# Transform products and transposes on 128x32 tiles, with two moves in the order of VectorE and ScalarE

## The chip, the cores and the metric

The kernel runs on one core of a Trainium2 chip. The metric is the device time of one execution in microseconds (us). A core has five engines that work side by side, each through its own queue in order: TensorE (PE in the profile, its weight loads apart as PEld), VectorE (DVE), ScalarE (ACT), GpSimd (POOL) and SyncE (SP). POOL and SP mostly issue DMA transfers here. All data is fp32.

## The reference

Input x is 8 images of 32 channels and 128 x 128 pixels. Two layers follow one another, each with a normalisation of channel pairs ahead and a residual sum behind:

```
layer 0:  g  = groupnorm(x)                           16 groups of two channels
          for 25 offsets in a 5x5 window: cost = 3x3 box sum of sum_c (g - shifted g)^2
          idx = the 8 offsets of least cost, per pixel
          xb  = the 8 shifted copies of g              256 channels, c*8 + k
          dct = for each c: 8x8 matrix over k of xb    (a grouped 1x1 convolution)
          h   = relu(dw3x3(W1 xb));  h = relu(dw3x3(W3 h));  w = sigmoid(dw3x3(W5 h))
          x1  = x + Wagg * (grouped 8->1 of (w * dct))
layer 1:  out = x1 + conv5x5(groupnorm(x1))            one 5x5 kernel for all channels
```

W1, W3 and W5 are 256 x 256; dw3x3 is a convolution of each channel with its own 3x3 kernel. "Transform" below is the line dct, "convolution 1, 2, 3" the three pairs of a 1x1 and a 3x3 convolution.

## The kernel before

An image goes through in 16 strips of R = 8 rows, with one further round (n = 16) that empties the pipeline. The main loop runs over 136 steps (8 images x 17), and each step has four stages in the order i = 3, 2, 1, 0: convolution 3 of strip s-2, convolution 2 of strip s-1, convolution 1 of strip s, and the transform and final sum of strip s-2. The 256 channels lie as two tiles of 128 partitions.

*A convolution.* The upper 128 channels are done on VectorE: `pointwise_v` makes the 1x1 products (pv, in PSUM), ScalarE copies them to tv (L678), ScalarE makes the first of nine taps (L722) and VectorE the other eight as multiply-adds of 128 x 1024 elements (L725); ScalarE applies the activation (L729). `depthwise_v` is a generator for this: its successive `next` calls give the first tap, the eight multiply-adds, the activation, and the DMA that moves the last two rows to the top for the next strip (`rows_before_v`, on SP). The lower 128 channels are done on TensorE: `pointwise_t` (p), ScalarE's copies to t (L701), row copies on SP (L707, L709), and `depthwise_t` makes the 3x3 convolution as products with small diagonal weights (pw, L751), with the activation in the copy out (L764).

*The order.* PE, DVE and ACT take their instructions in the order in which the program calls them; it is written by hand in the main loop. `new_v` is the generator of the running stage, `dv` that of the stage before, `kept` that of the one before that. So the activation of convolution 1 is issued at the end of stage 0 (`next(dv, None)`), and its row copy in stage 3 of the next step (`next(kept, None)`). The block matching for the next image (squares of differences on DVE and ACT, df; sums on PE, pd; the 8 best by MAX8 and FIND_INDEX8, L536 and L537; indices, oc) is cut into small tasks in queues "D", "A", "P" and "Q"; `tick` takes a share of the D tasks in each stage.

*The gather.* Each stage builds one selection: POOL loads indices (ib, L602), ScalarE makes one-hot rows in two passes (sel, L616 and L617), and PE multiplies them with pixels (pg, L631), copied to xb (L638) and from there to DRAM (xbd, L640).

*Transform and final sum.* `final_load` (at the end of stage 0, for the next step) brings the residual rows xr and the matched strips xf back from DRAM. For xf it issues eight DMAs of 32 partitions (L791), so that the partitions are ordered by the half of the channels; xf has one buffer, so the load waits for the last reader. `final_dct` multiplies xf with ldct in 64 x 64 quadrants: four products fill the quadrants for four rows of both tiles, eight for a full strip (pc, L810). VectorE multiplies the convolution 3 result by them (L818). In the next step `final_add` makes the products pa with the aggregation weights (L831), VectorE adds xr (L839) and takes statistics (L840), and POOL stores the rows (L844).

*PSUM.* pv, p, pg, pc, pa and the transposes share the pool ps_x of five buffers, handed out in turn; pc takes four of them in a full step. pw and pd have their own.

*Transposes.* Pixels (px, L407, four per group, 64 groups), costs (pt, L525, the same) and indices (pi, L569, 64 singly) are turned by TensorE's transpose of 128 x 128 tiles.

Of the kernel before, what the change touches and what calls it, by code (L numbers as in the profile page):

```python
# [8 lines left out]
F32 = mybir.dt.float32  # L9
# [7 lines left out]
P = 128  # L17
C, K, H, W = 32, 8, 128, 128
# [18 lines left out]
C_M32 = C_G2 + 32  # L37
# [7 lines left out]
def bm3d_conv_preact(  # L45
# [16 lines left out]
    nc = tc.nc  # L62
# [41 lines left out]
    lw5 = const.tile([P, 2, CK], F32, name="lw5")  # L104


    ldct = const.tile([P, 2, 64], F32, name="ldct")
    lagg = const.tile([P, 2, C], F32, name="lagg")


# [89 lines left out]

    queues = {"B": deque(), "D": deque(), "A": deque(), "P": deque(), "Q": deque()}

# [94 lines left out]
    def mixes():  # L300

        dq = work.tile([P, 2, K], F32, name="dq", tag="dq", bufs=1)
        src = dct_w.rearrange("(m h c i) k a b -> m h k c (i a b)", m=2, h=2, i=K)
        for k in range(K):
            for m in range(2):
                for h in range(2):
                    p = 64 * h + 32 * (k % 2) + 8 * (k // 2)
                    nc.sync.dma_start(dq[p : p + 8, m], src[m, (h + m + 1) % 2, k])
        m8 = work.tile([P, 8], F32, name="m8", tag="m16", bufs=1)
        yield "D", 1.0, 10  # L310
        nc.vector.tensor_reduce(
            m8,
            cst[:, C_M32 : C_M32 + C].rearrange("p (a c) -> p c a", c=8),
            axis=mybir.AxisListType.X,
            op=ALU.add,
        )
        for m in range(2):
            nc.vector.tensor_tensor(
                ldct[:, m].rearrange("p (c i) -> p c i", i=K),
                m8.unsqueeze(2).to_broadcast([P, 8, K]),  # L320
                dq[:, m].unsqueeze(1).to_broadcast([P, 8, K]),
                ALU.mult,
            )

# [74 lines left out]
    def sources(b, xn):  # L399
# [3 lines left out]
        for r in range(0, 32, 4):  # L403
            yield "P", 0
            pt = ps_x.tile([P, 4, P], F32, name=f"px_{b}_{r}", tag="x")
            for q in range(4):
                nc.tensor.transpose(pt[:, q], xn[:, 3 + r + q, 2 : 2 + W], ident)  # L407
            xs = work.tile([P, 4, P], F32, name=f"xs_{b}_{r}", tag="ct")
            nc.scalar.copy(xs, pt)
            for q in range(4):  # L410
                nc.gpsimd.dma_start(
                    xl.rearrange("(g r) x c -> r x g c", g=4)[r + q],
                    xs[:, q].rearrange("p (g c) -> p g c", c=C),
                )
# [70 lines left out]
    def costs(b, i, sq, idx):  # L485
# [35 lines left out]
        for h in range(0, R, 4):  # L521
            yield "P", 0
            pt = ps_x.tile([P, 4, P], F32, name=f"pt_{b}_{i}_{h}", tag="x")
            for q in range(4):
                nc.tensor.transpose(pt[:, q], cost[:, h + q], ident)  # L525
# [16 lines left out]
    def places(b, idx, i):  # L542
# [23 lines left out]
        yield "P", 0  # L566
        for h in range(2):
            pt = ps_x.tile([P, 512], F32, name=f"pi_{b}_{i}_{h}", tag="x")
            nc.tensor.transpose(pt[:, :P], o[:, h * P : (h + 1) * P], ident)  # L569
# [141 lines left out]
    def depthwise_v(i, b, n):  # L711
# [4 lines left out]
        for k, (dy, dx) in enumerate(  # L716
# [4 lines left out]
            if k == 0:  # L721
                nc.scalar.activation(acc, rows, AF.Copy, scale=tap)  # L722
                yield out_
            else:
                nc.vector.scalar_tensor_tensor(  # L725
                    acc, rows, tap, acc, op0=ALU.mult, op1=ALU.add
                )
# [42 lines left out]
    def final_load(b, n):  # L770
# [24 lines left out]

    def final_dct(b, n, acc, xf, j0, j1):

        for r0 in range(0, R, 4):
# [5 lines left out]
            pc = [  # L804
                ps_x.tile([P, 4, W], F32, name=f"pc_{b}_{n}_{m}_{r0}", tag="x") for m in range(2)
            ]
            for h in range(2):
                for m in range(2):
                    o = 64 * ((h + m + 1) % 2)
                    nc.tensor.matmul(  # L810
                        pc[m][o : o + 64, : z - a],
                        ldct[64 * h : 64 * h + 64, m],
                        xf[64 * h : 64 * h + 64, m, a:z],
                        start=True,
                        stop=True,
                    )
# [219 lines left out]
    with tc.manual_schedule(engines=ORDERED):  # L1036
# [19 lines left out]
        for s in range(len(steps) + 2):  # L1056
# [10 lines left out]
            for i in (3, 2, 1, 0):  # L1067
# [111 lines left out]
```

## Time and profile before

| | |
|---|---|
| median of 3 runs | 6524.21 us (6519.26 to 6526.59) |
| the profiled execution | 6526.97 us, its span 6525.2 us |
| TensorE's granted clock over the span | 0.979 of full speed |
| busy: PE / PEld / DVE / ACT / POOL | 6180.3 / 3262.3 / 5856.5 / 5051.0 / 3077.3 us |
| multiply-adds of the convolutions on VectorE (L725) | 4031.6 us, 3264 instructions |
| transform products (L810, pc) | 272.0 us of 64x512, 1984 records |
| transpose products px, pt, pi | 42.6, 44.5, 15.5 us |
| xf loads issued by POOL (L791) | 651.0 us, 1088 instructions |

Columns of a group in the profile: line, engine, operation, output <- input with buffer numbers left out, partitions x elements, count, then busy time, mean of one in ns, and the idle time of the engine just before, with the instruction that ended most of it. For products the partitions are given as rows * columns of the part of the array in use (128*32 is 128 rows by 32 columns). Products overlap, so the mean of one is longer than what it adds. The list of waits has the waiting line, the line waited for, us in total, times, and the longest. The view of stretches gives the length of each, and the busy time of each engine in it.

### The profile page before, as it was taken

To read this page: it belongs to the slowest core of one execution; us is meant where nothing else is said; L and a number is where in the kernel's file an instruction comes from. 1 tells how busy PE (TensorE), PEld (TensorE's weight loads), DVE (VectorE), ACT (ScalarE), POOL (GpSimd) and SP (SyncE) were. 2 spreads that over 40 slices of the span, in tenths; PEclk is the share of its full clock that TensorE was granted. 3 is DMA by queue.
4 is the path that set the end of the run, shared out by engine and by line. 5 is a ranking of instruction groups with operands and counts; after the bars stand their busy time and mean duration, and the time that the engine had idled before them with its cause. 6 is when DMAs were issued, how large, how long until landed. Compare 5 with 4: busy or idle time off the path is not lost.

```text
span 6525.2 us, 234180 instructions
## 1 busy us (share of the span) xinstructions
PE 6180.3 (95%) x102306; PEld 3262.3 (50%) x102306; DVE 5856.5 (90%) x8828; ACT 5051.0 (77%) x6698; POOL 3077.3 (47%) x5015
## 2 busy tenths in 40 slices
PE   5799999999999999999999999999999999999997
PEld 1445445544555546454555544544545454465553
DVE  7899988999889998899998999899998999988776
ACT  5787769778787877877778787887869787787772
POOL 8345436444364444643446534454345644344334
PEclk7899999999999999999999999999999999999998
DMA  4555555565555655655546556565555665455553
GB/s 85 125 135 144 123 124 146 145 143 135 133 145 139 142 147 127 150 140 135 141 129 157 140 131 151 127 150 137 139 134 138 150 147 133 118 149 147 137 135 79
DMA packets 544960, 886.21 MB, mean 136 GB/s; under 512 B 248880, under 2 KB 312944, under 8 KB 543936
## 3 DMA queue, kind: packets, MB, share of 16 engines
q0 software_dynamic: 383648, 611.87, 37.4%
q1 hardware_dynamic: 157776, 258.11, 16.4%
q8 instruction: 805, 13.19, 0.9%
q10 hardware_dynamic: 2512, 1.25, 0.1%
q14 instruction: 219, 1.79, 0.1%
HBM read 420.60 MB, written 216.49 MB: 98 GB/s over the span
## 4 chain that ended last, share of the span: by engine, by line
PE 50%; DVE 32%; ACT 5%; POOL 5%; DMA 4%; issue 4%; SPq 0%; ACTq 0%; DVEq 0%; POOLq 0%
DVE acc L725 21%; PE pw L751 16%; PE pv L670 12%; PE p L694 11%; PE pg L631 4%; DVE idx L537 3%; POOL xtd L424 3%; PE pc L810 2%; DVE df L444 2%; DVE acc L818 1%; PE p L924 1%; DVE mx L536 1%; PE pd L459 1%; DMA t<-t 1%; ACT sel L616 1%
## 5 line engine op out<-in xcount | busy, mean ns | idle before, releaser
L725 DVE SCALAR_TENSOR_TENSOR acc<-tv,dwv,acc 128x1024 f32<-128x1024 f32 (+3 forms) x3264 | 4031.6, 1237 | 156.3 <-ACT acc L722 52.0
L751 PE MATMUL pw<-t,dwd 96*32 96x254 f32 (+7 forms) x31680 | 2118.1, 419 | 23.0 <-DMA t<-t 10.1
L751 PEld LDWEIGHTS pw<-t,dwd 96*32 96x32 f32 (+1 forms) x31680 | 1105.7, 110 | 826.8 <-issue 369.3
L616 ACT ACTIVATE sel<-ib,nplace 128x1024 f32<-128x1024 uint8 x1024 | 1170.8, 1143 | 62.0 <-DMA ib<-idxd 62.0
L617 ACT ACTIVATE sel<-sel 128x1024 f32<-128x1024 f32 x1024 | 1086.0, 1061 | 32.5
L670 PE MATMUL pv<-acc,lw 128*32 128x512 f32 x8448 | 959.8, 590 | 54.4 <-DVE acc L818 47.8
L694 PE MATMUL p<-acc,lw 128*32 128x256 f32 x16768 | 974.3, 379 | 2.2 <-issue 2.2
L602 POOL DMA_DIRECT2D ib<-idxd x512 | 292.0, 570 | 1207.3 <-ACT sel L616 1078.1
L791 POOL DMA_DIRECT2D xf<-xbd x1088 | 651.0, 632 | 279.9 <-PE pc L810 180.6
L694 PEld LDWEIGHTS p<-acc,lw 128*32 128x32 f32 x16768 | 570.7, 111 | 393.6 <-issue 67.4
L729 ACT ACTIVATE acc<-acc 128x1024 f32<-128x1024 f32 (+3 forms) x408 | 417.1, 1022 | 390.2 <-DVE acc L725 389.8
L678 ACT COPY tv<-pv 128x512 f32<-128x512 f32 (+2 forms) x784 | 435.9, 579 | 338.5 <-PE pv L670 334.1
L631 PE MATMUL pg<-sel,xt 120*32 120x88 f32 (+1 forms) x24576 | 611.7, 244 | 64.8 <-ACT sel L617 56.1
L631 PEld LDWEIGHTS pg<-sel,xt 120*32 120x32 f32 x24576 | 559.5, 111 | 219.2 <-ACT sel L617 74.4
L670 PEld LDWEIGHTS pv<-acc,lw 128*32 128x32 f32 x8448 | 290.2, 110 | 532.3 <-issue 409.7
L764 ACT ACTIVATE acc<-pw 128x512 f32<-128x512 f32 (+2 forms) x808 | 436.6, 572 | 133.4 <-PE pw L751 131.8
L444 DVE TENSOR_TENSOR df<-xn 128x786 f32<-128x786 f32 (+2 forms) x576 | 530.4, 972 | 2.2 <-PE pd L459 1.9
L701 ACT COPY t<-p 128x512 f32<-128x512 f32 x800 | 421.7, 571 | 115.4 <-PE p L694 115.4
L452 ACT ACTIVATE df<-df 128x786 f32<-128x786 f32 (+2 forms) x576 | 458.9, 859 | 50.0 <-DVE df L444 48.6
L722 ACT ACTIVATE acc<-tv,dwv 128x1024 f32<-128x1024 f32 (+3 forms) x408 | 455.1, 1115 | 42.3 <-PE pa L831 24.8
L670 PE MATMUL pv<-xb,lw 128*32 128x512 f32 x4096 | 470.8, 596 | 0.0
L694 PE MATMUL p<-xb,lw 128*32 128x256 f32 x8192 | 469.9, 380 | 0.0
(155 smaller groups left out, 5893.0 us busy)
## 6 DMA issues: line engine op xcount, KB each, us to landing
ib<-idxd POOLq DMA_DIRECT2D x512, 256.0 KB, 4.0
xbd<-xb POOLq DMA_DIRECT2D x128, 1024.0 KB, 6.0
xf<-xbd POOLq DMA_DIRECT2D x960, 128.0 KB, 6.8
t<-t SPq DMA_DIRECT2D x792, 128.0 KB
t<-t SPq DMA_DIRECT2D x384, 256.0 KB
tv<-tv SPq DMA_DIRECT2D x384, 130.0 KB
xt<-xtd POOLq DMA_DIRECT2D x240, 180.0 KB, 4.0
xtd<-xl POOLq DMA_DIRECT2D x192, 96.0 KB, 3.3
```

Source lines behind the costliest of these rows:

```text
L444: nc.vector.tensor_sub(df[:, :, ca:cz], xn[:, r0 : r0 + SR, ca:cz], xn[:, r0 + dy : r0 + dy + SR, ca + dx : cz + dx],)
L452: nc.scalar.activation(df[:, :, ca:cz], df[:, :, ca:cz], AF.Square)
L616: nc.scalar.activation(sel, ib, AF.Square, bias=nplace)
L617: nc.scalar.activation(sel, sel, AF.Relu, scale=-1.0, bias=1.0)
L631: nc.tensor.matmul(pg[C * j : C * (j + 1), :, :, xa:xz], xt[: 8 * QW, f * (NT // 2) + t], sels[j // 2][: 8 * QW, j % 2 * 2 : j % 2 * 2 + 2 ...
L670: nc.tensor.matmul(ps[C * j : C * (j + 1), :hr], lhsT[:, g, P + C * j : P + C * (j + 1)], src(g)[:, h : h + hr], start=g == 0, stop=g == 1,)
L694: nc.tensor.matmul(ps[C * r : C * (r + 1), e, :nb], lhsT[:, g, s], rows[:, r : r + 4 * nb - 3 : 4], start=g == 0, stop=g == 1,)
L722: nc.scalar.activation(acc, rows, AF.Copy, scale=tap)
L725: nc.vector.scalar_tensor_tensor(acc, rows, tap, acc, op0=ALU.mult, op1=ALU.add)
L751: nc.tensor.matmul(pt[u][C * j : C * (j + 1), ka:kz, :nb, xa:xz], dwd[0:hi, i - 1, u, j, dx + 1], t[0:hi, j, ka:kz, :nb, xa + dx : xz + dx ...
L764: nc.scalar.activation(rows[:, u : u + 2 * nh[u] - 1 : 2, :nb], pt[u][:, : nh[u], :nb], funcs[i - 1])
L791: nc.gpsimd.dma_start(xf[p : p + C, m, j0:j1], src[g, m, (h + m + 1) % 2, :, :, ya:yz])
```

## The change

There are four parts. (1) The transform is made with 128 x 32 column tiles: ldct holds the whole 128 x 128 block matrix of a tile, xf is loaded in the order of xbd's partitions with two DMAs of 128 partitions, and each of two tiles and four column blocks is one product over all 128 rows. (2) The transposes of px, pt and pi become four ordinary products each, with 32 columns of the data as weights and the identity as the moving operand. (3) In convolution 1, the multiply-adds stop after six; the transform's VectorE products come next, and then the last two multiply-adds. (4) Convolution 1's activation is issued in stage 3 of the next step, right behind the first tap of convolution 3, and not at the end of stage 0.

```diff
-    ldct = const.tile([P, 2, 64], F32, name="ldct")
+    ldct = const.tile([P, 2, P], F32, name="ldct")
...
+    def transpose(out_, in_):
+        for j in range(0, P, C):
+            nc.tensor.matmul(out_[j : j + C], in_[:, j : j + C], ident, start=True, stop=True)
...
     def mixes():
-        src = dct_w.rearrange("(m h c i) k a b -> m h k c (i a b)", m=2, h=2, i=K)
+        src = dct_w.rearrange("(m c i) k a b -> m k c (i a b)", m=2, i=K)
         for k in range(K):
             for m in range(2):
-                for h in range(2):
-                    p = 64 * h + 32 * (k % 2) + 8 * (k // 2)
-                    nc.sync.dma_start(dq[p : p + 8, m], src[m, (h + m + 1) % 2, k])
+                p = 32 * (k // 2) + k % 2
+                nc.sync.dma_start(dq[p : p + 31 : 2, m], src[m, k])
...
-                nc.tensor.transpose(pt[:, q], xn[:, 3 + r + q, 2 : 2 + W], ident)
+                transpose(pt[:, q], xn[:, 3 + r + q, 2 : 2 + W])
...
-                nc.tensor.transpose(pt[:, q], cost[:, h + q], ident)
+                transpose(pt[:, q], cost[:, h + q])
...
-            nc.tensor.transpose(pt[:, :P], o[:, h * P : (h + 1) * P], ident)
+            transpose(pt[:, :P], o[:, h * P : (h + 1) * P])
...
     def depthwise_v(i, b, n):
             else:
+                if i == 1 and k == 7:
+                    yield
                 nc.vector.scalar_tensor_tensor(
...
     def final_load(b, n):
-        src = xbd[b].rearrange("(j m h c) g y x -> g m h j c y x", j=4, m=2, h=2)
+        src = xbd[b].rearrange("(j m c) g y x -> m j (c g) (y x)", j=4, m=2)
         for m in range(2):
-            for h in range(2):
-                for g in range(2):
-                    p = 64 * h + C * g
-                    nc.gpsimd.dma_start(
-                        xf[p : p + C, m, j0:j1], src[g, m, (h + m + 1) % 2, :, :, ya:yz]
-                    )
+            nc.gpsimd.dma_start(
+                xf[:, m, j0:j1].rearrange("p y x -> p (y x)"), src[m, :, :, W * ya : W * yz]
+            )
...
     def final_dct(b, n, acc, xf, j0, j1):
-            for h in range(2):
-                for m in range(2):
-                    o = 64 * ((h + m + 1) % 2)
+            for m in range(2):
+                for q in range(4):
+                    s = slice(C * q, C * (q + 1))
                     nc.tensor.matmul(
-                        pc[m][o : o + 64, : z - a],
-                        ldct[64 * h : 64 * h + 64, m],
-                        xf[64 * h : 64 * h + 64, m, a:z],
+                        pc[m][s, : z - a],
+                        ldct[:, m, s],
+                        xf[:, m, a:z],
                         start=True,
                         stop=True,
                     )
...
                     accs[i, bi, ni] = [None, next(new_v)]
+                if i == 3:
+                    next(kept, None)
                 next(later, None)
...
                     final_dct(bi, ni, accs[3, bi, ni], xf, j0, j1)
+                if not i:
+                    next(dv, None)
...
                 run("A")
-                next(dv, None)
+                if i:
+                    next(dv, None)
```

In the main loop's stage 0 `dv` is the generator of convolution 1, so the new `next(dv, None)` issues its last two multiply-adds behind `final_dct`; in stage 3 of the next step `kept` is the same generator, and the new `next(kept, None)` issues its activation, the old one its row copy. Convolutions 2 and 3 keep their order.

More of the change, by code (lines that the diff above doesn't have):

```diff
@@ L302, in mixes @@
         dq = work.tile([P, 2, K], F32, name="dq", tag="dq", bufs=1)
-        src = dct_w.rearrange("(m h c i) k a b -> m h k c (i a b)", m=2, h=2, i=K)
+        src = dct_w.rearrange("(m c i) k a b -> m k c (i a b)", m=2, i=K)
         for k in range(K):
             for m in range(2):
-                for h in range(2):
-                    p = 64 * h + 32 * (k % 2) + 8 * (k // 2)
-                    nc.sync.dma_start(dq[p : p + 8, m], src[m, (h + m + 1) % 2, k])
-        m8 = work.tile([P, 8], F32, name="m8", tag="m16", bufs=1)
+                p = 32 * (k // 2) + k % 2
+                nc.sync.dma_start(dq[p : p + 31 : 2, m], src[m, k])
+        m16 = work.tile([P, 16], F32, name="m16", tag="m16", bufs=1)
         yield "D", 1.0, 10
         nc.vector.tensor_reduce(
-            m8,
-            cst[:, C_M32 : C_M32 + C].rearrange("p (a c) -> p c a", c=8),
+            m16,
+            cst[:, C_M32 : C_M32 + C].rearrange("p (c g) -> p c g", g=2),
             axis=mybir.AxisListType.X,
@@ L319, in mixes @@
                 ldct[:, m].rearrange("p (c i) -> p c i", i=K),
-                m8.unsqueeze(2).to_broadcast([P, 8, K]),
-                dq[:, m].unsqueeze(1).to_broadcast([P, 8, K]),
+                m16.unsqueeze(2).to_broadcast([P, 16, K]),
+                dq[:, m].unsqueeze(1).to_broadcast([P, 16, K]),
                 ALU.mult,
```

## The prediction

> **What bounds the kernel now.** I read first the page's engine row and its chain, then TensorE's own timeline of one step with the products' shapes, then what TensorE waits for, and last the steps one by one. From the page:
>
> ```profile
> span 6525.2 us, 234180 instructions
> ...
> PE 6180.3 (95%) x102306; PEld 3262.3 (50%) x102306; DVE 5856.5 (90%) x8828; ACT 5051.0 (77%) x6698; POOL 3077.3 (47%) x5015
> ...
> PE 50%; DVE 32%; ACT 5%; POOL 5%; DMA 4%; issue 4%; SPq 0%; ACTq 0%; DVEq 0%; POOLq 0%
> ```
>
> TensorE leaves 345 us of the span open, VectorE 669; the chain changes between the two. TensorE's timeline of a step (start, length, group; a group runs on for some 0.2 us under the next, so its cost is start to next start):
>
> ```profile
> 3004.51 3.63 PE L670 MATMUL pv<-acc,lw 128*32 128x512 f32 x32
> 3007.94 0.86 PE L459 MATMUL pd<-df,neg 128*32 128x396 f32 x8
> ...
> 3018.17 3.64 PE L670 MATMUL pv<-xb,lw 128*32 128x512 f32 x32
> 3021.75 0.66 PE L525 MATMUL pt<-cst,dsum 128*128 128x128 f32 x4
> 3022.34 3.66 PE L694 MATMUL p<-xb,lw 128*32 128x256 f32 x64
> ...
> 3026.76 5.31 PE L751 MATMUL pw<-t,dwd 96*32 96x512 f32 x48
> 3032.00 1.95 PE L810 MATMUL pc<-xf,ldct 64*64 64x512 f32 x16
> 3033.88 0.86 PE L459 MATMUL pd<-df,neg 128*32 128x393 f32 x8
> ...
> 3042.17 3.64 PE L670 MATMUL pv<-acc,lw 128*32 128x512 f32 x32 [1.32 <-DVE acc L818]
> ```
>
> To see: the line of pv has 16 products of the code as 32 records, two per fp32 product, and takes 3.43 us from start to next start: eight rounds of four records, 0.43 us each. The transform, pc, has 8 products, 16 records, in 1.88 us: four rounds of 0.43 and a rest. What pv waits for in the last line is a result buffer: pc holds four of the five x buffers until VectorE's multiplications (L818) have read them, and these stand behind eight multiply-adds of convolution 1:
>
> ```profile
> 3031.01 10.51 DVE L725 SCALAR_TENSOR_TENSOR acc<-tv,dwv,acc 128x1024 f32<-128x1024 f32 x8
> 3041.43 2.47 DVE L818 TENSOR_TENSOR acc<-acc,pc 128x512 f32<-128x512 f32 x4
> ```
>
> TensorE's waits from 230 to 6420 us (before that VectorE and ScalarE prepare image 0, after it the last image is finished):
>
> ```profile
> PE pv L670 <- DVE acc L818: 47.8, 28, 3.6
> PE pg L631 <- ACT sel L617: 46.9, 28, 2.2
> PE pi L569 <- DVE oc L560: 31.6, 10, 8.6
> PE pc L810 <- ACT t L701: 12.3, 7, 2.4
> ```
>
> By the stretches of that view TensorE's open time is 109 us before 230, 45 after 6420 and 191 between; only the 191 can be won here. Then each step of image 3, from pc to the next pc (length, then busy time of TensorE, weight loads, VectorE):
>
> ```profile
> 2937.10:2987.10 50.00, 50.00 (x821) 24.18 (x820) 41.69 (x47) 38.88 (x51) 18.57 (x27) 1.00 0.53 126
> ...
> 3032.00:3080.60 48.60, 45.40 (x778) 23.10 (x774) 47.09 (x80) 37.63 (x50) 13.11 (x24) 1.00 0.49 121
> ...
> 3218.10:3268.20 50.10, 45.31 (x755) 23.49 (x754) 48.27 (x105) 34.72 (x47) 21.27 (x38) 0.97 0.61 141
> ...
> sum 791.80, PE 766.63 PEld 406.73 DVE 729.18 ACT 630.06 POOL 382.65; mean PE 45.10 PEld 23.93 DVE 42.89 ACT 37.06 POOL 22.51
> ```
>
> The first step is TensorE's alone: no gap, and VectorE has 8 us over. In the other two VectorE waits for nothing; its 1.5 to 1.8 us beside the busy time are the small gaps between its instructions. TensorE is the limit in most steps, VectorE in about five of seventeen.
>
> **The change, part by part.** *Transform.* pc becomes 16 products of 128 rows by 32 columns, over all 128 rows though only 32 of them carry weights for a block of columns: 32 records of 128x512, the very shape of pv, so 3.43 us. Now it costs 1.88 plus its way in: the pw group ahead takes 5.24 us to pc's start, where the 96-record group with the same columns takes 5.16 (3013.01 to 3018.17), so 0.1. That is +1.45 per full step. The way in and out of the 64*64 tiles (0.1, and 1.88 - 4 x 0.43 = 0.16) is all that the new shape saves; the four extra rounds are 1.72. There are 8 x 15 full steps: 174 us. The first step of an image (5 rows) has 5/8 of the rounds, +0.8; the last (3 rows) +0.37: 9 us. Sum 183.
>
> *Transposes.* A group of four pt or px is 4 records now, 0.59 us, plus 0.15 on its way in (3018.17 to 3021.75 is 3.58, against 3.43). As ordinary products it is 16 products, 32 records, eight rounds of 128 columns. The nearest row is pw 96*32 with 128 columns, 48 records from 2583.94 to 2585.39: 0.12 per round with a change of tiles in it; half of pw's 0.215 for 256 columns is 0.108. So 0.86 to 0.97 against 0.74; I take +0.15. 128 groups: 19 us. The 64 single pi come out even. TensorE's work grows by 202 us.
>
> The row shows 0.1 to 0.16 us lost at each change between 64*64 or 128*128 and 128*32. The Trainium skill, TensorEngine Tiling (Array Packing), Key Properties, says that a change of tiling mode, not of tile, drains the engine: that is the rule for this change. Against it stands the same page's Gotcha 2, that column tiling excludes the transpose mode for fp32, which agrees with the doubled records of the transposes. TensorE: Matmul & The Clock Gate, Back-to-back issue gap, gives 518 cycles for 512 columns, 216 ns at its 2.4 GHz; an estimate by that page makes the extra rounds half as dear, some 90 us. The trace has 430 ns a round here, and decides.
>
> *Products behind six multiply-adds.* VectorE's work is the same, in another order: L818 stands 2 x 1.3 = 2.6 us earlier. With pc 1.45 us longer, the pv behind it asks some 4 us later for a buffer than it does now, relative to L818; the longest wait there is 3.6. So the 47.8 us go, nearly all. What can be late instead is pc itself: in steps that TensorE leads, VectorE comes to L818 2.6 us sooner and finds the second pair 1.5 us later. That puts up to some 2 us of waiting on VectorE and, queued behind, taps 7 and 8 and the block-matching pieces. VectorE has it to spare there: it waits 261.2 us for pa at L839 now, and will wait there less.
>
> *Activation.* L729 of convolution 1 holds ScalarE's queue at the step's end (L729 waits 389.8 us for L725 in all), and sel, the last pw copies and the next pv copies stand behind. It moves behind the next pv copies and the first tap of convolution 3. There 1.06 us of it come before sel and the t copies; its reader, pv of convolution 2, follows pa, p and pg: 0.9 + 3.4 + 0.9 us after the pv ahead, against some 3 us for copy, tap and L729. So it is in time, with 2 us over. Where VectorE is the limit, ScalarE may wait up to 2 us there for taps 7 and 8; it waited up to 9.2 at the old place. The sel waits of TensorE lose 1.06 of at most 2.2, and pc covers 1.45: most of the 46.9 go. The SP queue's row copy of convolution 1 waits for taps 7 and 8, so starts up to 2.6 us later; its reader is three stages off.
>
> *Loads of xf.* Two DMAs per step for eight, the same bytes and 4 KB pieces. POOL issues six fewer of 0.632 us: 500 us off an engine 47% busy, worth nothing by itself; ib may be issued earlier (ScalarE waits 62 us for ib in all, the gain's upper end; the lower is a large load holding ib up by one landing of 6.8 us now and then). I take 0. Setting up the weights has 16 DMAs fewer on SP, hidden in the first 230 us behind image 0's preparation.
>
> *The sum.* I set each step to the larger of TensorE's busy time plus its increase, and VectorE's busy time plus 1.5. This drops every wait of TensorE that is not VectorE's own pace. For image 3: 50.0 becomes 51.6, 48.6 and 50.1 stay within 0.4 us, and the seventeen sum to 798.2 against 791.8, +6.4, from a gross 25.5. The same rule gives +2.2, 4.7, 5.0, 5.6, 6.6 and 11.4 for images 0, 1, 2, 4, 5 and 6, and +16.3 for the last, where little block matching is left and TensorE has only 6 us of waits. Together +58. Waits that are neither product buffers nor sel (pc for ScalarE's copies 19, transfers and issue 15) and some of pi's will partly stay: I add 25. So +83 on the profiled execution, 6527.0 us with what lies around its span (2.8 above the median of the runs): 6610, or 6607 against the median. I say 6605.
>
> **Rivals.** *The waits stay.* TensorE pays the whole 202 and only the buffer wait goes: +154, 6680; with nothing won, 6725. For it: sel and pi waits come from queues that the change loads as before. Against: a longer TensorE gives ScalarE and VectorE 1.45 us more per step to be ready.
>
> *VectorE averages out, not slower.* The rule takes each step alone. If, with the buffers free 2.6 us earlier, TensorE may run ahead over two or three steps, heavy and light steps even out and all 191 us go: 202 - 191 = +11, 6535. It decides if TensorE's waits between 230 and 6420 us fall under some 10 us. Against it: pa, the copies and xr tie the engines together in each step, and now the kernel is 12 us per image longer than the larger of the two engines, step by step.
>
> *The new order makes a wait.* If L729 at its new place, or L818 waiting for pc, holds up the t copies or the taps in VectorE's five steps per image, 2 us x 5 x 8 = 80 us come on top of 58 + 25: 6690.
>
> *No extra rounds.* If the four column tiles of pc ran in the time of the quadrants, only +20 for the transposes would be left, and the won waits would make it about 6400. The pv row with the same shape excludes it; I give it next to nothing.
>
> **How the numbers follow.** Forecast (6560 to 6650) 0.62; waits stay 0.13; new wait 0.10; averaging out 0.13; no extra rounds 0.02. The range for eight in ten runs from just above the averaging case, 6537, to 6680. 0.2% is 13 us, about what a measurement of this kernel can tell: faster (below 6511) 0.06, same 0.07, slower 0.87.
>
> **What would show it.** pc with 32 records of 128x512 at 3.4 us a step; TensorE's busy time near 6380 us; px and pt near 0.9 us; "pv L670 <- DVE acc L818" gone; L729's wait for L725 well under 390 us; VectorE's busy time unchanged and its waits larger. It is wrong if TensorE's waits between 230 and 6420 us do not fall from 191 to about 70, or if pc costs other than 3.4 us.

## The result and the profile after

The changed kernel takes 6677.0 us in the median (6672.1 to 6695.9) against 6523.6 of the kernel before: a ratio of 1.0241 [1.0220, 1.0262], 153 us slower. The forecast was 6605, +81, most likely between 6560 and 6650 and with eight chances in ten between 6537 and 6680: the sign is right, the size misses by 72 us. The profiled execution took 6674.1 us, its span 6672.3.

The page of the kernel after, its engine row and its chain:

```profile
span 6672.3 us, 245344 instructions
...
PE 6361.0 (95%) x108450; PEld 3852.5 (58%) x108450; DVE 5859.9 (88%) x8828; ACT 5060.3 (76%) x6698; POOL 2633.6 (39%) x4199
...
PE 71%; DVE 9%; DMA 7%; ACT 5%; POOL 4%; issue 4%; ACTq 0%; SPq 0%; POOLq 0%; DVEq 0%
```

TensorE is busy for 181 us more, VectorE for as long as before. In the chain TensorE has 71% for 50, VectorE 9% for 32, and the transfers have 7% for 4: they are waited for more than before.

TensorE's timeline of the kernel after, the same stretch of work as the one shown of before:

```profile
3032.93 3.62 PE L673 MATMUL pv<-xb,lw 128*32 128x512 f32 x32
3036.36 1.06 PE L206 MATMUL pt<-cst,dsum 128*32 128x128 f32 x32
3037.23 3.64 PE L697 MATMUL p<-xb,lw 128*32 128x256 f32 x64
3041.63 5.31 PE L756 MATMUL pw<-t,dwd 96*32 96x512 f32 x48
3046.76 3.62 PE L812 MATMUL pc<-xf,ldct 128*32 128x512 f32 x32
```

pc has 32 records of 128x512, as forecast. A like line of pc 52 us earlier runs 3.44 us to the next start (2994.93 to 2998.37). The pw ahead takes 5.13 us to pc's start, where it took 5.24: +1.56 - 0.11 = +1.45 per step, to the hundredth what the working had. pt takes 0.87 and costs nothing more on its way in (pv ahead 3.43): +0.13 where +0.15 was taken.

What waits in the kernel after (waiting line, line waited for, us in total, times, longest), from the list of waits:

```profile
DVE acc L820 <- PE pc L812: 120.3, 174, 6.3
ACT sel L619 <- DMA ib<-idxd: 86.9, 15, 13.1
POOL x1d L846 <- DMA xf<-xbd: 82.9, 17, 11.2
ACT acc L734 <- DVE acc L730: 73.2, 50, 5.9
PE pc L812 <- DMA xf<-xbd: 25.5, 7, 4.4
```

The same waits in the kernel before, whose list has no line of pc for xf (its 0.8 us show only in the narrower view from 230 to 6420 us):

```profile
ACT acc L729 <- DVE acc L725: 389.8, 159, 9.2
ACT sel L616 <- DMA ib<-idxd: 62.0, 14, 10.3
POOL x1d L844 <- DMA xf<-xbd: 54.3, 56, 4.5
DVE acc L818 <- PE pc L810: 10.5, 10, 3.6
```

The third and the last line of the kernel after bear on the chain: pc now waits for the load of xf, which it hardly did before, and POOL, whose queue also issues other loads and stores, is held by it for 82.9 us at L846 alone (54.3 before). All of POOL's lines that wait for a landing of xf sum to 285 us, against 98 before. VectorE waits 120.3 us for pc (10.5 before), ScalarE 86.9 for the indices ib (62.0). The activations wait 73.2 us for VectorE's multiply-adds, where they waited 389.8, and "pv <- acc", 47.8 us before, is 0.7. So both moves took away the waits that they were made for.

One step shows it whole. First the POOL queue of the kernel after, then TensorE, at the second step of image 3:

```profile
2771.29 0.74 POOL L643 DMA_DIRECT2D xbd<-xb  x1
2771.91 0.83 POOL L793 DMA_DIRECT2D xf<-xbd  x1
2772.61 0.71 POOL L605 DMA_DIRECT2D ib<-idxd  x1
...
2778.16 0.62 POOL L502 DMA_DIRECT2D dsum<-sq  x1 [1.83 <-DMA xbd<-xb]
2785.37 6.47 POOL L502 DMA_DIRECT2D dsum<-sq  x11 [6.59 <-DMA xf<-xbd]
```

```profile
2780.42 1.12 PE L812 MATMUL pc<-xf,ldct 128*32 128x512 f32 x8
2785.23 1.06 PE L812 MATMUL pc<-xf,ldct 128*32 128x512 f32 x8 [3.68 <-DMA xf<-xbd]
2788.45 3.64 PE L812 MATMUL pc<-xf,ldct 128*32 128x512 f32 x16 [2.16 <-ACT t L704]
```

The second load of xf is issued at 2771.9. TensorE has done the first tile's products of the first four rows at 2781.5 and waits 3.68 us for the second tile, which lands some 13 us after its issue. POOL, which waits for the same landing, issues nothing for 6.59 us. This step takes 62.0 us, where its counterpart took 57.8. In the mean over images 1 to 6, an image grows by 16.0 us (786.1 to 802.1); this second step has 4.6 of it, the fourth 3.2 and the eleventh 3.4. A step that TensorE leads and no load is late for grows by the forecast 1.4 (40.0 to 41.4 in the mean of the thirteenth).

The reason is in the transfers, by the page's list of DMA issues (KB each, median us from issue to landing), first before, then after:

```profile
xbd<-xb POOLq DMA_DIRECT2D x128, 1024.0 KB, 6.0
xf<-xbd POOLq DMA_DIRECT2D x960, 128.0 KB, 6.8
x1d<-xr POOLq DMA_DIRECT2D x480, 32.0 KB, 3.4
```

```profile
xbd<-xb POOLq DMA_DIRECT2D x128, 1024.0 KB, 14.5
xf<-xbd POOLq DMA_DIRECT2D x240, 512.0 KB, 12.9
x1d<-xr POOLq DMA_DIRECT2D x480, 32.0 KB, 6.3
```

xf lands after 12.9 us for 6.8, and two stores that the change does not touch land later as well: xbd 14.5 for 6.0, x1d 6.3 for 3.4.

### The profile page after: what moved, and what is told of

It is laid out like the page before. It is cut to its first block, busy times and chain, and to the rows that moved or that the text cites. A ratio compares the mean times of both kernels' runs of the same rounds, so it can differ in the third digit from the quotient of the medians.

```text
span 6672.3 us, 245344 instructions
## 1 busy us (share of the span) xinstructions
PE 6361.0 (95%) x108450; PEld 3852.5 (58%) x108450; DVE 5859.9 (88%) x8828; ACT 5060.3 (76%) x6698; POOL 2633.6 (39%) x4199
## 4 chain that ended last, share of the span: by engine, by line
PE 71%; DVE 9%; DMA 7%; ACT 5%; POOL 4%; issue 4%; ACTq 0%; SPq 0%; POOLq 0%; DVEq 0%
PE pw L756 24%; PE pv L673 16%; PE p L697 15%; PE pc L812 6%; PE pg L634 5%; DVE acc L730 5%; DMA ib<-idxd 2%; DMA t<-t 2%; POOL xtd L427 2%; PE p L926 2%; DMA xf<-xbd 2%; PE pd L462 1%; PE pa L833 1%; DVE idx L540 1%; ACT sel L619 1%
## 5 line engine op out<-in xcount | busy, mean ns | idle before, releaser
L756 PE MATMUL pw<-t,dwd 96*32 96x254 f32 (+7 forms) x31680 | 2128.6, 418 | 43.0 <-DMA t<-t 18.9
L756 PEld LDWEIGHTS pw<-t,dwd 96*32 96x32 f32 (+1 forms) x31680 | 1252.2, 110 | 705.9 <-issue 336.9
L619 ACT ACTIVATE sel<-ib,nplace 128x1024 f32<-128x1024 uint8 x1024 | 1174.5, 1147 | 86.9 <-DMA ib<-idxd 86.9
L697 PE MATMUL p<-acc,lw 128*32 128x256 f32 x16768 | 990.4, 380 | 4.4 <-issue 4.4
L697 PEld LDWEIGHTS p<-acc,lw 128*32 128x32 f32 x16768 | 671.0, 111 | 297.9 <-issue 46.7
L634 PEld LDWEIGHTS pg<-sel,xt 120*32 120x32 f32 x24576 | 596.7, 110 | 155.1 <-issue 52.1
L634 PE MATMUL pg<-sel,xt 120*32 120x88 f32 (+1 forms) x24576 | 625.1, 243 | 44.5 <-ACT sel L620 30.2
L673 PEld LDWEIGHTS pv<-acc,lw 128*32 128x32 f32 x8448 | 350.3, 110 | 439.8 <-issue 335.0
L812 PE MATMUL pc<-xf,ldct 128*32 128x512 f32 (+2 forms) x4224 | 493.3, 599 | 37.4 <-DMA xf<-xbd 25.5
L846 POOL DMA_DIRECT2D x1d<-xr x544 | 279.7, 527 | 582.2 <-DVE xr L841 459.8
## 6 DMA issues: line engine op xcount, KB each, us to landing
xbd<-xb POOLq DMA_DIRECT2D x128, 1024.0 KB, 14.5
xf<-xbd POOLq DMA_DIRECT2D x240, 512.0 KB, 12.9
```

What stands on the lines that cost most here:

```text
L619: nc.scalar.activation(sel, ib, AF.Square, bias=nplace)
L634: nc.tensor.matmul(pg[C * j : C * (j + 1), :, :, xa:xz], xt[: 8 * QW, f * (NT // 2) + t], sels[j // 2][: 8 * QW, j % 2 * 2 : j % 2 * 2 + 2 ...
L673: nc.tensor.matmul(ps[C * j : C * (j + 1), :hr], lhsT[:, g, P + C * j : P + C * (j + 1)], src(g)[:, h : h + hr], start=g == 0, stop=g == 1,)
L697: nc.tensor.matmul(ps[C * r : C * (r + 1), e, :nb], lhsT[:, g, s], rows[:, r : r + 4 * nb - 3 : 4], start=g == 0, stop=g == 1,)
L756: nc.tensor.matmul(pt[u][C * j : C * (j + 1), ka:kz, :nb, xa:xz], dwd[0:hi, i - 1, u, j, dx + 1], t[0:hi, j, ka:kz, :nb, xa + dx : xz + dx ...
L812: nc.tensor.matmul(pc[m][s, : z - a], ldct[:, m, s], xf[:, m, a:z], start=True, stop=True,)
```

## The experiments

Three theories at the outset, by the letters that the expectations use. **A, the rounds:** TensorE's extra rounds are the loss, up to the 202 us of work that they add, and the moves win some of it back. **B, the moves:** the new order brings waits of its own that eat what it wins. **C, the loads:** the added work costs about what was forecast, and the 70 us that are missing come from the two loads of xf, which land late.

### The parts, one and two at a time

Four kernels: the kernel before with both moves alone; the changed kernel without the moves; the kernel before with the transform and its two loads alone; and with the transposes alone. The moves are these lines of the change:

```diff
+                if i == 1 and k == 7:
+                    yield
...
+                if i == 3:
+                    next(kept, None)
...
+                if not i:
+                    next(dv, None)
...
-                next(dv, None)
+                if i:
+                    next(dv, None)
```

> The kernel before with only the two moves in the order (the transform's VectorE products behind six multiply-adds, convolution 1's activation behind the next first tap); tiles, xf loads and transposes as before. Theory A (the loss is TensorE's extra rounds, the moves themselves win): the 47.8 us of pv waiting for L818 go and part of the sel waits, so 40 to 90 us below before, 6435 to 6485. Theory B (the moves bring new waits, VectorE at the transform's products above all, and eat what they win): within 20 us of before or above it. Theory C (the xf loads by two DMAs are the loss): same as A here.

> The changed kernel with the order of before: 128x32 tiles for the transform (with the two xf loads) and the transposes, nothing moved. Theory A: TensorE's busy time as in the changed kernel, near 6360, and the buffer waits come back in part, so 10 to 50 us above the changed kernel, 6685 to 6725. Theory B: without the moves the changed kernel gets faster, 6620 to 6670.

> Only the transform on 128x32 tiles with its two xf loads; order and transposes of before. Theory A: 183 us of TensorE work less what waits give back, 130 to 180 us above before, 6655 to 6705. Theory B as for the tiles run, less the transposes: above before by under 130. Theory C: the xf load shows as TensorE waits for the xf transfer of 25 us or more.

> Only the transposes as four ordinary products each; all else of before. Predicted 19 us of TensorE work; Theory A: 5 to 20 us above before. If a change of tiles costs more than the 0.15 us on the way in that was read from the trace, the time stays within 5 us of before.

Against 6526.5 us of the kernel before on that chip:

| kernel | us | ratio |
|---|---|---|
| both moves alone | 6531.6 | 1.0008 [0.9999, 1.0018] |
| change without the moves | 6674.9 | 1.0234 [1.0217, 1.0251] |
| transform with its two loads alone | 6665.5 | 1.0218 [1.0198, 1.0239] |
| transposes alone | 6534.1 | 1.0013 [1.0002, 1.0024] |

The transform with its loads carries 139 of the 153 us, the transposes 8, and the moves nothing, with or without it. Theory A had the moves win 40 to 90 us, so it fell on that point. The change without the moves lies between the ranges of A (6685 to 6725) and B (6620 to 6670). The transform alone lies in A's range, and TensorE waits 16.6 us for xf there, where C asked for 25 or more: the four runs do not yet tell the rounds from the loads. With the moves alone, pv's wait for its buffer falls from 47.8 to 18.1 us, but TensorE's busy time and span stay: part of the wait comes back as a wait for the next thing of VectorE. The list of waits of that kernel:

```profile
PE pv L670 <- DVE xr L841: 26.5, 18, 3.7
...
PE pv L670 <- DVE acc L820: 18.1, 7, 3.3
```

"pv <- xr" was 6.4 us before. In a step that VectorE leads, putting one of its instructions earlier puts another later; that this explains all of it is a reading of the waits.

### The loads and the rounds apart, and each move by itself

The eight loads in place of two in the changed kernel:

```diff
-            nc.gpsimd.dma_start(
-                xf[:, m, j0:j1].rearrange("p y x -> p (y x)"), src[m, :, :, W * ya : W * yz]
-            )
+            for j in range(4):
+                nc.gpsimd.dma_start(
+                    xf[C * j : C * (j + 1), m, j0:j1].rearrange("p y x -> p (y x)"),
+                    src[m, j, :, W * ya : W * yz],
+                )
```

The rounds alone: in the kernel before, pc's products are issued twice (the second writes the same values again).

```diff
-            for h in range(2):
+            for h in (0, 1, 0, 1):
```

The other two take from the moves' lines only the first and third (products behind six multiply-adds), or only the second and fourth as far as they place the activation.

> The changed kernel, but xf loaded by eight DMAs of 32 partitions and 128 KB, as many and as large as before. Theory C (the two 512 KB loads land late, 12.9 us after issue against 6.8, and TensorE waits 25.5 us for them, with ScalarE's later index loads behind): 25 to 50 us below the changed kernel, 6625 to 6650, and the pc wait for xf gone. Theory A (all of it is the extra rounds): within 10 us of the changed kernel.

> The kernel before, with the four products that fill the quadrants issued twice: the same result is written again. Four more rounds per step on TensorE, 1.72 us in a full step and 219 us in all, with tiles, loads and order of before. Theory A (rounds are the cause, and the waits give back only a part): as the transform alone cost 139 for 183 us of work, 219 cost 140 to 190, 6665 to 6715. Theory C (most of the loss is in the xf loads): under 110, below 6635.

> The kernel before with the first move alone: the transform's VectorE products behind six multiply-adds. The two moves together gave +5 us. If a wait that is taken away in a step that VectorE limits only turns up elsewhere in that step: within 15 us of before. If the moves cancel each other: 20 us or more below before here, and as much above in the run with the activation alone.

> The kernel before with the second move alone: convolution 1's activation behind convolution 3's first tap. If waits only move: within 15 us of before. If the moves cancel each other: 20 us or more above before, with ScalarE's copies or the selections late in stage 3.

Against 6525.2 us of before: eight loads 6593.4, 1.0107 [1.0090, 1.0124]; products twice 6634.2, 1.0168 [1.0151, 1.0185]; products behind six multiply-adds 6557.5, 1.0047 [1.0030, 1.0063]; the activation moved 6526.8, 1.0002 [0.9993, 1.0012].

Eight loads take back 84 of 153 us, more than the 25 to 50 that theory C expected, and xf lands earlier:

```profile
xf<-xbd POOLq DMA_DIRECT2D x960, 128.0 KB, 5.6
```

The rounds alone add 1.72 us of work per step, 219 us in all (gross: before anything of it is hidden), and cost 109, half of it; theory A had 140 to 190, C under 110. The first move alone costs 32 us, which neither of its expectations had (within 15 us, or 20 below). ScalarE's activations, still at their old place, wait longer for the multiply-adds, of which the last two now come later (389.8 us before):

```profile
ACT acc L731 <- DVE acc L727: 635.0, 174, 12.2
```

With both moves this wait is 133.0 us and the time that of the kernel before, so the second move takes back what the first costs.

### The size of the loads

> The changed kernel with xf loaded by four DMAs of 64 partitions (256 KB) instead of two of 512 KB; with eight it took 6593, with two 6677. Theory that the time goes with how late the last part of xf lands: the landing lies between the 5.6 us of eight and the 12.9 us of two, and the time between them, some 6620 to 6650. Rival that only the DMA over all 128 partitions is bad: the landing stays below 7 us and the time within 10 us of 6593. Rival that the number of POOL's issues matters: as two, within 10 us of 6677.

> The kernel before with the transform on 128x32 tiles alone, xf loaded by eight DMAs of 32 partitions; transposes and order as before. With two loads of 512 KB this transform took 6665.5. Theory that the loads cost the same with the order of before: 6665 - 84 = 6582, the transform's extra rounds alone some +55 to +65 of their gross 183. Rival that the two moves are what lets the eight loads win (the products wait until VectorE's six multiply-adds): 6610 to 6650.

> The kernel before with xf loaded by two DMAs of 128 partitions, 512 KB, as in the change, and its own 64x64 products. The channels then lie in another order than the products' weights, so the transform mixes wrong channels; work and shapes are those of before. It measures the loads by themselves. Theory that the late landing alone costs: pc waits for xf, and the time is 6526 + 50 to 90, 6576 to 6616. Rival that the loads cost only where the products are longer, or where each product needs all 128 rows: within 15 us of 6526.

> The kernel before with pc's products issued three times (twice took 6634, +109 of a gross 219). The third pass writes the same result again. Theory that the waits of TensorE give back a part once, and that VectorE's steps are few after the first addition: of the second 219 us some 180 to 219 show, 6815 to 6855; the rule step by step gives +253 against the kernel before, 6779. Rival that half of any added round is hidden: 6743.

The edit of the first, in the changed kernel:

```diff
-            nc.gpsimd.dma_start(
-                xf[:, m, j0:j1].rearrange("p y x -> p (y x)"), src[m, :, :, W * ya : W * yz]
-            )
+            for j in range(2):
+                nc.gpsimd.dma_start(
+                    xf[64 * j : 64 * (j + 1), m, j0:j1].rearrange("p y x -> p (y x)"),
+                    src[m, 2 * j : 2 * j + 2, :, W * ya : W * yz],
+                )
```

The second is the kernel before with the transform of the change and the eight loads above; the third is before with the two loads of the change in `final_load`; the fourth has `for h in (0, 1, 0, 1, 0, 1):` for pc.

Against 6525.7 us of before: four loads of 256 KB 6743.0, 1.0336 [1.0319, 1.0353]; the transform alone with eight loads 6581.5, 1.0089 [1.0072, 1.0106]; the kernel before with two loads 6591.4, 1.0097 [1.0068, 1.0127]; the products three times 6794.9, 1.0414 [1.0396, 1.0432].

Three readings. The two loads cost 66 us in the kernel before, with its own products and its own order (they land after 13.3 us there): this loss belongs to the loads and needs neither longer products nor products over all 128 rows. The transform with eight loads costs 56, as the theory of the loads had it (55 to 65). And four loads of 256 KB are the worst of all, outside each of the three expectations: 6743, worse than two of 512 KB, with nearly the same landing, 12.5 us for 12.9, at half the size:

```profile
xbd<-xb POOLq DMA_DIRECT2D x128, 1024.0 KB, 12.1
xf<-xbd POOLq DMA_DIRECT2D x480, 256.0 KB, 12.5
```

So the theory so far, late because large, fell. The third pass of the products costs 161 of its 219 us, less than the 180 to 219 expected; the step by step rule of the prediction gives 71 for two passes and 253 for three, and the runs are 38 and 16 us above it.

### How a load is spread

What the loads differ in besides size is the outermost dimension of the access in DRAM. The change reads "m j (c g) (y x)" with j outermost, 4 entries; the four loads of 256 KB take j in pairs, 2 entries; the eight loads of the experiment take one j each, so that (c g), 32 entries, is outermost; the kernel before reads "j c y x", again 4. A load whose outermost dimension has 16 entries or more is called spread below. Three kernels change the loads to that. In the changed kernel, still with two loads of 512 KB, the eight rows of a channel pair lie side by side in xf, so that (c g), 32 entries, is outermost; the weights' rows move with them:

```diff
-                p = 32 * (k // 2) + k % 2
-                nc.sync.dma_start(dq[p : p + 31 : 2, m], src[m, k])
+                p = 4 * (k % 2) + k // 2
+                nc.sync.dma_start(dq[p : p + 121 : 8, m], src[m, k])
...
-            cst[:, C_M32 : C_M32 + C].rearrange("p (c g) -> p c g", g=2),
+            ident.rearrange("p (c g) -> p c g", g=K),
...
-        src = xbd[b].rearrange("(j m c) g y x -> m j (c g) (y x)", j=4, m=2)
+        src = xbd[b].rearrange("(j m c) g y x -> m (c g) j (y x)", j=4, m=2)
```

The kernel before gets four loads of 256 KB in place of eight, in the same manner (its weights' rows moved likewise):

```diff
-        src = xbd[b].rearrange("(j m h c) g y x -> g m h j c y x", j=4, m=2, h=2)
+        src = xbd[b].rearrange("(j m h c) g y x -> m h (c g) j (y x)", j=4, m=2, h=2)
         for m in range(2):
             for h in range(2):
-                for g in range(2):
-                    p = 64 * h + C * g
-                    nc.gpsimd.dma_start(
-                        xf[p : p + C, m, j0:j1], src[g, m, (h + m + 1) % 2, :, :, ya:yz]
-                    )
+                nc.gpsimd.dma_start(
+                    xf[64 * h : 64 * h + 64, m, j0:j1].rearrange("p y x -> p (y x)"),
+                    src[m, (h + m + 1) % 2, :, :, W * ya : W * yz],
+                )
```

> The changed kernel, its two loads of 512 KB kept, but xf's partitions in another order (the eight of a channel pair side by side), and the weights' rows with them. The two DMAs have the same bytes, count and 4 KB pieces; their outermost dimension in DRAM has 32 entries, where that of the change has 4, that of the four loads of 256 KB had 2 and that of the eight loads of 128 KB 32. Theory that this dimension sets on how many DMA engines a load runs: the landing falls from 12.9 to 8 us or less, and the time to 6580 to 6605. Rival that it is the bytes of a DMA or the burst that they make: landing 11 to 13 us, 6665 to 6690.

> The kernel before with xf by four loads of 256 KB in place of eight of 128 KB, the partitions in an order that gives each load an outermost dimension of 16 entries, the weights' rows with them; 64x64 products as before. By the theory of the outermost dimension (before's own loads have one of 4) the landing is 6.8 us or less for twice the bytes, and the time that of before or up to 15 us less: 6511 to 6527. By the rival of the DMA's size it lands like the four loads of the changed kernel (12.5 us) and costs 40 us or more: 6565 or above.

> The kernel before with those four loads and both moves in the order (convolution 1's last two multiply-adds behind the transform's, its activation behind the next first tap). Theory that the moves only shift waits: within 10 us of the run with the four loads alone. Rival that the moves win the waits for pc's buffers and sel once xf is early: 15 to 40 us below it.

Against 6523.0 us of before: the change with the two loads spread 6593.4, 1.0106 [1.0089, 1.0122]; the kernel before with four spread loads 6504.6, 0.9974 [0.9963, 0.9986]; the same with both moves 6504.4, 0.9969 [0.9957, 0.9982]. The lists of DMA issues of the first two:

```profile
xbd<-xb POOLq DMA_DIRECT2D x128, 1024.0 KB, 7.1
xf<-xbd POOLq DMA_DIRECT2D x240, 512.0 KB, 5.6
x1d<-xr POOLq DMA_DIRECT2D x480, 32.0 KB, 2.5
```

```profile
xbd<-xb POOLq DMA_DIRECT2D x128, 1024.0 KB, 6.4
xf<-xbd POOLq DMA_DIRECT2D x480, 256.0 KB, 6.2
x1d<-xr POOLq DMA_DIRECT2D x480, 32.0 KB, 3.0
```

The same 512 KB land after 5.6 us, not 12.9, and the 84 us are gone. The four spread loads beat the kernel before by 18 us, a little more than the 15 expected at most: twice its bytes per DMA land a little sooner than its own. The moves add nothing to them.

The packets show what happened. The page gives the packets of the POOL queue, and how many of the core's are under 512 bytes; the change, then the same with its loads spread:

```profile
DMA packets 531688, 886.87 MB, mean 133 GB/s; under 512 B 235632, under 2 KB 299696, under 8 KB 530624
...
q0 software_dynamic: 370336, 611.82, 36.6%
```

```profile
DMA packets 434408, 886.45 MB, mean 134 GB/s; under 512 B 138288, under 2 KB 202352, under 8 KB 433344
...
q0 software_dynamic: 273056, 611.40, 33.3%
```

The same data, with 97,280 packets fewer on the queue, and 97,344 fewer under 512 bytes. Counted in words of 4 bytes from that queue's packet records of 4, 8, 12 and 16 bytes, the queue has 103,264 words with eight spread loads per step (1,088 in all) and 90,208 with two (272): 13,056 words over 816 DMAs, 16 per DMA, if a spread load has the same number in both. That leaves 85,856 for everything else on the queue, and for the loads of xf (a piece is one partition's run of a load, 4 KB in a full step):

| kernel | loads | outermost entries | KB per load | words per load | pieces per busy engine | landing, us |
|---|---|---|---|---|---|---|
| before | 8 | 4 | 128 | 112 = 16 + 12 x 8 | 8 | 6.8 |
| change | 2 | 4 | 512 | 400 = 16 + 12 x 32 | 32 | 12.9 |
| change, four loads | 4 | 2 | 256 | 464 = 16 + 14 x 32 | 32 | 12.5 |
| change, eight loads | 8 | 32 | 128 | 16 | 2 | 5.6 |
| change, two spread | 2 | 32 | 512 | 16 | 8 | 5.6 |
| before, four spread | 4 | 16 | 256 | 16 | 4 | 6.2 |

The two rows that gave the 16 fit by construction; the other four are the test, and their counts give whole numbers of words per load. All six fit a load that runs on 4, 4, 2, 16, 16 and 16 of the 16 engines, each idle one getting one word for each 4 KB piece that a busy one carries. The Trainium skill, DMA: Bandwidth & Descriptors, section "Why a DMA increments its semaphore by 16 and not by 1", states the rule: the number of engines is the largest up to 16 that divides the size of the slowest dimension on both sides. This case agrees in all six rows, by the counts and the landings. What the words are is inferred from the counts.

The semaphores show the number of engines without the words. Each load leaves 16 updates of its semaphore in the trace. For the load of the changed kernel issued at 2771.9 us, twelve come 4.0 to 6.3 us after the issue and the other four at 11.6 to 13.2; for its counterpart with spread loads all 16 come at 7.0 to 7.9. In the run with four loads of 256 KB, one issued at 1542.0 us has fourteen updates by 2.0 us and two at 10.8 and 11.2. So four and two are late, as many as the engines that the words give. (126 of the 272 loads of the change have eight late ones. 111 of these were issued less than 1.5 us behind another load of xf, and none of the 140 with four late ones was; the other four may be the engines still busy with the load ahead, which is not shown.)

With a busy engine carrying 8 pieces or fewer, a load lands after 5.6 to 6.8 us; with 32, after 12.5 or 12.9. As an estimate: a 4 KB packet took 0.246 us in the mean of the changed kernel's records, so 24 pieces more are 5.9 us, and 5.6 + 5.9 = 11.5 of the 12.9 measured.

## Why the prediction was right or wrong

*Loads of xf, "I take 0": the step that failed.* It compared the bytes and the 4 KB pieces of two DMAs with those of eight, found them equal, and gave "a large load holding ib up by one landing of 6.8 us now and then" as the lower end. Measured, by the same kernel with the two loads spread: 6677.0 - 6593.4 = 84 us. The number of DMAs went down to a quarter, and the number of engines on which each runs, by the words (and in the change by the semaphore updates too), stayed at 4, so each busy engine's share of a load went from 8 pieces to 32. One row of the trace, 6.8 us for 128 KB, was taken for the landing of any load of xf; it was that of a 128 KB load on four engines. The same list had a hint that was passed over: ib, 256 KB, landed after 4.0 us and the store xbd, 1024 KB, after 6.0, both sooner than the 128 KB of xf. And the cost was not ib alone: pc, xbd's and x1d's stores and every issue of POOL that waits for a landing of xf were held up (POOL's waits for xf, 285 us in the change, sum to 30 with the loads spread).

*TensorE's added work: right per step, less in the total.* pc is 32 records, 3.44 us, +1.45 a step; pt +0.13. The forecast gross was 202 us; TensorE's busy time rose by 181 (predicted "near 6380", measured 6361.0). The remaining 21 us were not traced. In the runs with pc two and three times the busy time also rose by less than was added (186 of 219 and 371 of 438), while the granted clock of the span rose from 0.979 to 0.983 and 0.988; in the change it is 0.980, as an estimate 0.1% of 6180 us, or 6 of the 21.

*The sum, +58 by the rule and +25 for waits that stay: near in size once the loads are set aside, in part by luck.* The comparison that comes nearest to holding the loads equal is the change with spread loads against the kernel before with spread loads: 6593.4 - 6504.6 = 89 us, forecast 83. The windows of these two profiles, the stretch between image 0's start and the last image's end in each, show of what it is made (length, then busy time of TensorE; first the change as it stands, then the change and the kernel before, both with spread loads):

```profile
230.00:6567.00 6337.00, 6180.21 (x106278) 3760.46 (x106274) 5631.90 (x8170) 4917.60 (x6490) 2425.60 (x3907) 0.99 0.54 135
```

```profile
230.00:6494.00 6264.00, 6152.19 (x106214) 3690.57 (x106210) 5627.32 (x8161) 4910.56 (x6486) 2376.29 (x3900) 0.99 0.51 137
```

```profile
230.00:6393.00 6163.00, 5984.59 (x100566) 3169.84 (x100562) 5619.74 (x8157) 4907.48 (x6485) 2527.50 (x4168) 0.99 0.54 139
```

With the loads spread in both, TensorE's busy time rises by 168 us and its waits fall from 178 to 112: 66 us of the added time are taken from waits. The forecast had 202 of work and waits from 191 to about 70, 121 less. Both terms were forecast too large, by 34 and 55 us, and most of that cancels in the sum; the waits that stay were priced too low even with early loads. (These two profiled executions lie 101 us apart, the medians 89.) In the changed kernel as it stands the waits fall from 191 only to 157 (6337.0 - 6180.2), and the prediction had named this as the sign that it is wrong ("do not fall from 191 to about 70"). Of the 73 us between it and the change with spread loads in these windows, 45 are waits of TensorE and 28 are longer busy time for the same products, at a granted clock of the span of 0.980 for 0.984; as an estimate from these clocks, 0.4% of 6180 us is 25. Pure rounds, with nothing moved, came out at 109 for 71 by the rule, and 269 for 253: 38 and 16 us above the rule, where the forecast added 25.

*Products behind six multiply-adds, "the 47.8 us go, nearly all": the wait went, the time did not.* It is 0.7 us in the changed kernel and 18.1 with the moves alone, and the time is the same with and without. By the lists of waits, a wait of TensorE for VectorE is in part only renamed in VectorE's steps. The rule had this right, since it let no step be shorter than VectorE; the paragraph on the move did not. VectorE's wait for pa was to shrink from 261.2 us; it is 271.0 in the changed kernel and 221.1 with the moves alone.

*Activation, "most of the 46.9 go": half wrong.* In the stretch in which it was 46.9 us, the wait for sel is 21.3 us in the changed kernel, but 43.5 with the moves alone. Over the whole span it is 56.1 before, 52.7 with the activation moved alone, and 36.2 with the products twice and nothing moved: longer products shorten it, the move hardly does. L734's wait is 73.2 us, as forecast well under 390. Alone, the move is worth 0 us; its worth is to undo the 32 us that the first move costs by itself, which the prediction did not see: the activations wait 635.0 us when taps 7 and 8 come later and the activation stays where it was.

*Transposes, 19 gross:* +8 us alone.

*Rivals.* "The waits stay" had the right time, 6680, for another reason: with the loads spread the waits do give way. "VectorE averages out" fell: 112 us of waits are left even with early loads. "A new wait" named L729 and L818. L818's wait for pc did grow, from 10.5 us to 120.3, but it grows to 55.8 with the moves alone, which cost no time; the wait that cost was at the load of xf.

## What to carry to other kernels

When a change merges DMAs, work out for the old and the new access what the outermost dimension is on both sides and how many engines it lets the load run on; equal bytes and equal pieces did not tell the landing here. A small load that lands later than larger transfers of the same queue is a sign to look for. Read the landing column for every transfer on the same queue, not only for the one changed: here an untouched store went from 6.0 to 14.5 us. And where two engines are tied together step by step, price added work by the larger of the two in each step, and give a reordering nothing unless the step's other engine has time left: the two moves together won nothing in three settings here.

## What was not expected of the hardware

The spread of a load can be read from its small packets: 16 words of 4 bytes for a load that runs on all engines, 112 to 464 for one that does not, with whole numbers of words per load in all six kernels, two of which set the scale. The late updates of a load's semaphore give the same number of engines. Half the size on half the engines lands just as late (12.5 against 12.9 us), so halving the load by its outermost dimension won nothing here, and cost 66 us more. Where these 66 us come from was not settled; its profile has more waits of POOL for xf at x1d (204.5 us for 82.9) and of TensorE's pw for row copies on another queue (43.4 for 18.9).
